# Self-attention over four 64x64 images on one Trainium2 core: the next image's v loaded by halves of a unit over 26 steps instead of by units over 16

## The chip, the cores and the metric

One core of one Trainium2 chip. The metric is the device time in microseconds from launch to end, the median of several runs. Nothing else runs on the chip beside it.

## The reference, cut to what matters

The input `x` has the shape (4, 64, 64, 256): four images, N = 4096 positions, C = 256 channels, all float32.

```python
q = einsum('bwhc,cd->bwhd', x, Wq) + bq        # 128 channels
k = einsum('bwhc,cd->bwhd', x, Wk) + bk        # 128 channels
v = einsum('bwhc,cd->bwhd', x, Wv) + bv        # 256 channels
pq, pk, pv = (t.reshape(B, -1, N) for t in (q, k, v))
energy = einsum('bcn,bcm->bnm', pq, pk)        # 4096 x 4096 for each image
attention = softmax(energy, axis=-1)
out = einsum('bcm,bnm->bcn', pv, attention).reshape(B, W, H, C)
return gamma * out + x
```

## The kernel before, in words

The order of all the work is written out by hand. After a prologue that projects image 0, one loop runs over n = 0 to 511. A step n stands for image b = n // 128, group g = (n % 128) // 16 (512 of the 4096 columns n of the reference) and unit t = n % 16 (256 of the 4096 rows m). So an image has 8 groups of 16 steps, and all 16 units of v are used once in each group, in the order of t.

**Precision.** Every operand of a large product is cut into three float32r forms h, l and d, and each product is three matmul passes. So k, q and v are stored as three forms each.

**What a step does on TensorE.** `cross(n + 2)` (line 369) begins the energies of two steps ahead, `attend(n, 0)` (line 443) multiplies the first 128 channels of v's unit t with the exponentials of step n, `energy(n + 2)` (line 384) finishes the energies, and `attend(n, 1)` does the other 128 channels. The results gather in four PSUM banks, a0, b0, a1 and b1, over the 16 steps of a group. Beside it ScalarE makes the exponentials (387) and the h forms (393), and VectorE the l and d forms (419, 421) and the row sums (404).

**The next image's projection** is spread over the same loop while there is a next image: `step(p, engine)` does the piece of one of 8 pairs of tiles. Its k, q and v forms are stored to DRAM (`kf`, `qd`, `vf`) on SP's queue by `store()`. During image 3 there is nothing left to project.

**Where v lives.** `vall` holds all 16 units of one image in SBUF: unit t has two halves i, each 128 partitions x 3 forms x 256 channels. When an image ends, its units are overwritten one by one with those of the next image out of `vf`, by `load_v` on GpSimd's queue. One half is 384 KB. Unit t of the old image is last read in step 128b - 16 + t, and unit t of the new image first in step 128b + t.

**Other transfers on GpSimd's queue.** `load_k(n + 5)` (line 356), 384 KB in each step, into one of three buffers: it waits for TensorE to be done with the buffer's old content, which is `energy(n + 2)` of the same step, and is read by `cross(n + 5)`, three steps later. `load_q` (350), 768 KB at t = 8. And line 502: at t = 10 of the next group it adds the input to the finished output tile `o` with an accumulating transfer.

**How a group ends.** In the last step of a group, t = 15, `emptied(n, 0)` (line 463) copies a0 and b0 out of PSUM into the tile `o`, ScalarE's work; the two others follow in the next step. `o` has one buffer. `finish` is a generator that is advanced once in each step and carries `o` through the next group: row sums through DRAM and back (SP's queue, lines 469 to 495), the division (498), the accumulating load of x (502) and the store to `out` (505, SP's queue). So `emptied` of one group waits until the store of the group before has landed, and the next group's first `attend` waits until `emptied` has freed the banks.

The loads of v stand at the end of a step, behind that step's `load_k` in GpSimd's queue, and ahead of `proceed()`, which advances `finish`:

```python
            if n >= STEPS - NU + 3 and (n - 3) // NU % NG == NG - 1 and (n - 3) // STEPS + 1 < B:
                load_v((n - 3) // STEPS + 1, (n - 3) % NU)
            proceed()
```

So both halves of unit t are issued at the end of step 128b - 13 + t, three steps after the last use of the old unit and 13 steps ahead of the first use of the new one.

Of the kernel before, what the change touches and what calls it, by code (L numbers as in the profile page):

```python
# [20 lines left out]
def kernel(  # L21
# [36 lines left out]
    nc = tc.nc  # L58
    B, W, H, C = x.shape
# [24 lines left out]
    NG = N // NB  # L84
    NU = NM // 2
    STEPS = NG * NU
# [14 lines left out]
    with ExitStack() as fast:  # L101
# [14 lines left out]
        vall = qkv.tile([P, NU, 2, 3, C], F32R, tag="v", name="v")  # L116
# [28 lines left out]
        qd, kf, vf, units, loads, now = {}, {}, {}, {}, {}, {}  # L145
        active, stores = [], []

        def proceed():
            for pieces in list(active):
                if next(pieces, StopIteration) is StopIteration:  # L150
                    active.remove(pieces)
# [29 lines left out]
        def image(b):  # L181
            for g in range(NG):
                qd[b, g] = dram.tile([P, NJ, 3, P], F32, tag=f"qd{g}", name=f"qd_{b}_{g}")
            for t in range(NU):
                kf[b, t] = dram.tile([P, 2, 3, P], F32, tag=f"kf{t}", name=f"kf_{b}_{t}")
                vf[b, t] = dram.tile([P, 2, 3, C], F32, tag=f"vf{t}", name=f"vf_{b}_{t}")
# [13 lines left out]
        def load_x(b, i):  # L200
            if b == B or i >= NI:
                return
            if b == 0:
                t = xs4[:, i % 4]
                if i:
                    nc.sync.dma_start(t, xv[b, i])
                loads["x", b, i] = t
                return
            pair = work.tile([P, 2, 2, XB], F32, tag="xd", name=f"x_{b}_{i}", bufs=1)
            for u in range(2):  # L210
                nc.sync.dma_start(pair[:, u], xv[b, i + u])
                loads["x", b, i + u] = pair[:, u]
# [120 lines left out]
        def store():  # L333
            for to, f in stores:
                if to.dtype == F32R:
                    nc.gpsimd.dma_start(to, f)
                else:
                    nc.sync.dma_start(to, f.bitcast(F32))
            stores.clear()

        def load_v(b, t):
            for i in range(2):
                nc.gpsimd.dma_start(vall[:, t, i], vf[b, t][:, i])  # L343

        def q_tile(g, name, dtype=F32R):
            return work.tile([P, NJ, 3, P], dtype, tag=f"q{g % 2}", name=name, bufs=1)
# [1 line left out]
        def load_q(b, g):  # L348
            loads["q", b, g] = q_tile(g, f"q_{b}_{g}")
            nc.gpsimd.dma_start(loads["q", b, g], qd[b, g])  # L350

        def load_k(n):
            b, u = divmod(n, STEPS)
            if b < B:
                t = kpool.tile([P, 2, 3, P], F32R, tag="k", name=f"k_{b}_{u}")
                nc.gpsimd.dma_start(t, kf[b, u % NU])  # L356
                loads["k", n] = t
# [5 lines left out]
        def cross(n):  # L363

            if n >= B * STEPS:
                return
            for i in range(2):
                e = units["e", n, i] = ps_e.tile([P, NB], F32, tag="e", name=f"e_{n}_{i}")
                nc.tensor.matmul(e, *forms(n, i, 2), start=True, stop=False, skip_group_check=True)  # L369
                nc.scalar.mul(e, e, -REST)  # L370

        def energy(n):

            if n >= B * STEPS:
                return
            if n % NU:
                x = ppool.tile([P, 2, NB], F32, tag="x", name=f"x_{n}")
            else:
                x = ppool.tile([P, 2, NB], F32, tag="s", name=f"s_{n // NU}")
            units[n] = x  # L380
            for i in range(2):
                e = units.pop(("e", n, i))
                for f in range(2):
                    nc.tensor.matmul(  # L384
                        e, *forms(n, i, f), start=False, stop=(f == 1), skip_group_check=True
                    )
                nc.scalar.activation(x[:, i, :], e, AF.Exp, scale=(1.0 + E) ** 3 / E)  # L387

        def upper(n):
            if n >= B * STEPS:  # L390
                return
            h = ppool.tile([P, 2, NB], F32R, tag="h", name=f"h_{n}", bufs=3)
            nc.scalar.activation(h, units[n], AF.Identity, scale=UPPER)  # L393
            units[n] = units[n], h
# [36 lines left out]
        def attend(n, j, order=(0, 1, 2)):  # L431

            t = n % NU
            if t == 0:
                for i, c in enumerate("ab"):
                    pool, tag = ps_o, f"{c}{j}"
                    if j and n >= (B - 1) * STEPS and n // NU % 2 == 0:
                        pool, tag = now["banks"][i]
                    now[c, j] = pool.tile([P, NB], F32, tag=tag, name=f"{c}{j}_{n // NU}")
            for f in order:  # L440
                to = now["ab"[f == 2], j]
                for i in (1, 0) if f == 1 else (0, 1):
                    nc.tensor.matmul(  # L443
                        to,
                        vall[:, t, i, f, j * P : (j + 1) * P],
                        units[n][f][:, i, :],
                        start=(t == 0 and i == 0 and f != 1),
                        stop=(t == NU - 1 and f != 0 and i == f // 2),
                        skip_group_check=True,
                    )  # L450

        def emptied(n, j, banks=None, only=None, vector=False):

            if j == 0:
                now["o"] = work.tile([P, 2, 2, NB], F32, tag="o", name=f"o_{n // NU}", bufs=1)
            for c, scale in enumerate((gam2, gam1)):
                if only in (None, c):
                    y = banks[c] if banks else now["ab"[c], j]
                    to = now["o"][:, c, j, :]
                    if vector:  # L460
                        nc.vector.tensor_scalar(to, y, scale, None, ALU.mult)
                    else:
                        nc.scalar.activation(to, y, AF.Identity, scale=scale)  # L463
# [230 lines left out]
        for n in range(B * STEPS):  # L694
            b, u = divmod(n, STEPS)
            g, t = divmod(u, NU)
            final = n == B * STEPS - 1
            if n == 0:
                image(1)
                load_x(1, 0)  # L700
            if u == STEPS - 5 and b + 2 < B:
                image(b + 2)
            if n == B * STEPS - 6:
                xr = ppool.tile([P, 2, NB], F32, tag="s", name="xr")
                nc.sync.dma_start(xr, xg[b, g])
            cross(n + LOOK)
            turn = t == NU - 1 and not final
            if t == 0 and n:
                upper(n + LOOK - 1)
            p = n - 2 + (n > 17)  # L710
            step(p, "act")
            late = n >= (B - 1) * STEPS
            if not final:
                attend(n, 0)
            if late and 1 <= t <= 2 and n > 1:
                emptied(n - 1 - t, 1, done, t - 1)
            energy(n + LOOK)
            load_k(n + LOOK + 3)
            store()
            if t == 0 and n:  # L720
                done = full
            if turn:
                emptied(n, 0)
            else:
                upper(n + LOOK)
            step(p, "pe")
            if turn:
                active.append(finish(n // NU, now["o"], now["s"]))
            if t == 0 and n and not late:
                emptied(n - 1, 1, done, vector=True)  # L730
            halves(n + 1)
            step(p, "dve")
            if final:
                finish_last(n, xr)
                break
            attend(n, 1)
            full = now["a", 1], now["b", 1]
            if n == 17:
                for engine in ("act", "pe", "dve"):
                    step(p + 1, engine)  # L740
            if t == 8 and n + NU < B * STEPS:
                load_q(*divmod(n // NU + 1, NG))
            if n >= STEPS - NU + 3 and (n - 3) // NU % NG == NG - 1 and (n - 3) // STEPS + 1 < B:
                load_v((n - 3) // STEPS + 1, (n - 3) % NU)
            proceed()

    NB = 512
    NG = N // NB
    NJ = NB // P
    NP = NM // 2  # L750
    with tc.If(nc.values_load(again[0:1, 0:1]) > 0), ExitStack() as general:
# [91 lines left out]
        for b in range(B):  # L843
# [16 lines left out]
            for g in range(NG):  # L860
# [65 lines left out]
                r = work.tile([P, NB], F32, tag="r", name=f"gr_{b}_{g}")  # L926
# [36 lines left out]
```

## Time and profile before

| | |
|---|---|
| median of 3 runs | 2329.9 us (2328.8 to 2330.72) |
| the profiled execution's own time | 2329.92 us |
| its span, first to last instruction | 2328.0 us |
| PE / DVE / ACT / POOL busy | 99% / 93% / 77% / 18% of the span |
| granted TensorE clock | 0.999 |
| bytes moved by DMA | 445.30 MB, mean 191 GB/s |

PE is TensorE, PEld its weight loads, DVE VectorE, ACT ScalarE, POOL GpSimd and SP SyncE, which issues transfers only. In rows of the views, `x5` is a count, and an arrow in brackets tells the idle time just before an instruction and what ended it. A view of windows gives each engine's busy time in a stretch of the span. "Landing" of a transfer is the time from its issue until its semaphore tells that all bytes are there. The DMA share is the mean busy share of the 16 DMA engines; it can exceed 1, as packets overlap.

### The profile page before, as it was taken

How to read it: one execution, taken by the hardware profiler on the slowest of the kernel's cores; microseconds unless marked ns; L12 is line 12 of the kernel's file. 1: busy time of each engine (PE TensorE's matmuls, PEld its weight loads, DVE VectorE, ACT ScalarE, POOL GpSimd, SP SyncE). 2: the span in 40 equal slices, each digit the busy share in tenths (PEclk: the TensorE clock that was granted, in tenths of full speed). 3: DMA queues.
4: the chain of work that ended last, by engine and by line, in shares of the span. 5: the costliest groups of instructions: out<-in, count | busy, mean ns of one | idle time of the engine just before them, and what ended most of it. 6: DMA issues, size and time to landing. Idle time of an engine off the chain costs nothing.

```text
span 2328.0 us, 31989 instructions
## 1 busy us (share of the span) xinstructions
PE 2309.8 (99%) x10758; PEld 1934.2 (83%) x10758; DVE 2175.0 (93%) x2174; ACT 1797.0 (77%) x2917; POOL 417.3 (18%) x716
## 2 busy tenths in 40 slices
PE   9999999999999999999999999999999999999998
PEld 9888888888878888888888888888887888888887
DVE  8999999999999999999999999999999999888988
ACT  7778777787777777777777777777787788788875
POOL 7111111111321111111132111111113111111110
PEclk9999999999999999999999999999999999999999
DMA  8567765577985776666698567665579745545553
GB/s 266 162 168 210 205 177 155 168 208 200 298 249 167 208 203 180 166 168 195 201 319 246 167 188 206 198 167 167 169 226 332 206 135 142 146 133 149 154 151 97
DMA packets 232190, 445.30 MB, mean 191 GB/s; under 512 B 27986, under 2 KB 109652, under 8 KB 232020
## 3 DMA queue, kind: packets, MB, share of 16 engines
q0 software_dynamic: 101120, 280.54, 45.0%
q1 hardware_dynamic: 130352, 162.38, 20.9%
q8 instruction: 88, 1.44, 0.3%
q14 instruction: 82, 0.67, 0.1%
q10 hardware_dynamic: 548, 0.26, 0.0%
HBM read 321.92 MB, written 120.39 MB: 190 GB/s over the span
## 4 chain that ended last, share of the span: by engine, by line
PE 96%; DMA 3%; ACT 0%; DVE 0%; issue 0%; POOL 0%; ACTq 0%; DVEq 0%
PE a L443 39%; PE e L384 19%; PE b L443 19%; PE e L369 10%; PE qv L257 5%; PE v L274 3%; PE xt L219 1%; DMA out_dram<-o 1%; DMA o<-in_x_dram 1%; DMA k<-kf 1%; DMA rows<-in_L_conv_bk_dram 0%; ACT qv L292 0%; POOL v L343 0%; ACT o L463 0%; POOL k L356 0%
## 5 line engine op out<-in xcount | busy, mean ns | idle before, releaser
L387 ACT ACTIVATE x<-e 128x512 f32<-128x512 f32 x960 | 522.1, 596 | 323.2 <-PE e L384 323.1
L370 ACT ACTIVATE e<-e 128x512 f32<-128x512 f32 x1024 | 546.4, 571 | 135.3 <-PE e L369 135.3
L443 PE MATMUL a<-h,v 128*128 128x512 f32 x2048 | 634.6, 391 | 4.6 <-ACT o L463 4.6
L443 PE MATMUL a<-ld,v 128*128 128x512 f32 x2048 | 631.7, 390 | 0.0
L443 PE MATMUL b<-ld,v 128*128 128x512 f32 x2048 | 631.6, 390 | 0.0
L419 DVE TENSOR_TENSOR ld<-x,h 128x1024 fp32r<-128x1024 f32 x480 | 586.1, 1221 | 37.0 <-ACT h L393 21.0
L404 DVE TENSOR_TENSOR s<-s,x 128x1024 f32<-128x1024 f32 x480 | 585.6, 1220 | 35.2 <-ACT x L387 34.0
L356 POOL DMA_DIRECT2D k<-kf x512 | 272.4, 532 | 1847.9 <-PE e L384 1753.1
L421 DVE SCALAR_TENSOR_TENSOR ld<-h,x 128x1024 fp32r<-128x1024 f32 x480 | 585.6, 1220 | 0.0
L384 PE MATMUL e<-q,k 128*128 128x512 f32 x2048 | 548.1, 390 | 0.0
L393 ACT ACTIVATE h<-x 128x1024 fp32r<-128x1024 f32 x480 | 510.6, 1064 | 14.2
L443 PEld LDWEIGHTS a<-ld,v 128*128 128x128 f32 x2048 | 384.8, 188 | 80.3
L443 PEld LDWEIGHTS b<-ld,v 128*128 128x128 f32 x2048 | 384.7, 188 | 80.0 <-DVE ld L421 0.2
L384 PEld LDWEIGHTS e<-q,k 128*128 128x128 f32 x2048 | 384.6, 188 | 79.4
L443 PEld LDWEIGHTS a<-h,v 128*128 128x128 f32 x2048 | 379.8, 188 | 79.3 <-ACT o L463 5.5
L369 PE MATMUL e<-q,k 128*128 128x512 f32 x1024 | 316.2, 390 | 2.5 <-DMA k<-kf 2.5
L369 PEld LDWEIGHTS e<-q,k 128*128 128x128 f32 x1024 | 191.7, 188 | 43.3 <-ACT o L463 1.8
L310 DVE SCALAR_TENSOR_TENSOR f<-f,qv 128x512 fp32r<-128x512 f32 x128 | 86.1, 683 | 0.3
L419 DVE TENSOR_TENSOR ld<-s,h 128x1024 fp32r<-128x1024 f32 x32 | 39.2, 1226 | 46.6 <-ACT h L393 46.6
L257 PE MATMUL qv<-wf,xf 128*128 128x256 f32 x576 | 78.2, 287 | 0.2
L257 PEld LDWEIGHTS qv<-wf,xf 128*128 128x128 f32 x576 | 74.7, 193 | 3.1 <-issue 0.9
L165 DVE SCALAR_TENSOR_TENSOR vf<-vf,v 128x512 fp32r<-128x512 f32 x96 | 65.4, 682 | 0.5 <-ACT vf L155 0.4
(88 smaller groups left out, 1129.2 us busy)
## 6 DMA issues: line engine op xcount, KB each, us to landing
k<-kf POOLq DMA_DIRECT2D x512, 384.0 KB, 3.6
vf<-vf SPq DMA_DIRECT2D x96, 384.0 KB, 5.2
v<-vf POOLq DMA_DIRECT2D x96, 384.0 KB, 8.3
kf<-f SPq DMA_DIRECT2D x128, 192.0 KB, 3.6
qd<-f SPq DMA_DIRECT2D x124, 192.0 KB, 3.8
q<-qd POOLq DMA_DIRECT2D x31, 768.0 KB, 6.2
zd<-s SPq DMA_DIRECT2D x62, 256.0 KB, 4.9
y<-zd SPq DMA_DIRECT2D x248, 64.0 KB, 4.4
```

What stands on the lines that cost most here:

```text
L257: nc.tensor.matmul(to[:, s, :], left, right.rearrange("p s a -> p (s a)") if w else right, start=(f == 2 and s == k == 0), stop=(f == 1 an ...
L310: nc.vector.scalar_tensor_tensor(f[:, :, :, j, :], h.bitcast(F32), s, y, ALU.mult, op)
L356: nc.gpsimd.dma_start(t, kf[b, u % NU])
L369: nc.tensor.matmul(e, *forms(n, i, 2), start=True, stop=False, skip_group_check=True)
L370: nc.scalar.mul(e, e, -REST)
L384: nc.tensor.matmul(e, *forms(n, i, f), start=False, stop=(f == 1), skip_group_check=True)
L387: nc.scalar.activation(x[:, i, :], e, AF.Exp, scale=(1.0 + E) ** 3 / E)
L393: nc.scalar.activation(h, units[n], AF.Identity, scale=UPPER)
L404: nc.vector.tensor_tensor(s, s, x, ALU.add)
L419: nc.vector.tensor_tensor(l, x, h.bitcast(F32), ALU.subtract)
L421: nc.vector.scalar_tensor_tensor(d, h.bitcast(F32), 1.0 + E, x, ALU.mult, ALU.subtract)
L443: nc.tensor.matmul(to, vall[:, t, i, f, j * P : (j + 1) * P], units[n][f][:, i, :], start=(t == 0 and i == 0 and f != 1), stop=(t == NU - ...
```

## The change

`load_v` takes one half instead of a unit. Number the 32 halves m = 0 to 31, unit m // 2, half m % 2. Half m is now issued at the end of step 128b - 13 + (13 m // 16). The first half stands where it stood; the last, m = 31, stands at the end of step 128b + 12, which is t = 12 of the new image's first group, three steps ahead of its use at t = 15. A step issues one or two halves, 32 in 26 steps, where it was two in each of 16 steps. The number of transfers and their sizes stay: 96 of 384 KB for the three image changes. They keep their place within the step.

```diff
-        def load_v(b, t):
-            for i in range(2):
-                nc.gpsimd.dma_start(vall[:, t, i], vf[b, t][:, i])
+        def load_v(b, t, i):
+            nc.gpsimd.dma_start(vall[:, t, i], vf[b, t][:, i])
...
-            if n >= STEPS - NU + 3 and (n - 3) // NU % NG == NG - 1 and (n - 3) // STEPS + 1 < B:
-                load_v((n - 3) // STEPS + 1, (n - 3) % NU)
+            for m in range(2 * NU):
+                c, r = divmod(n + NU - 3 - 13 * m // 16, STEPS)
+                if r == 0 and 0 < c < B:
+                    load_v(c, m // 2, m % 2)
             proceed()
```

Line numbers below are those of the kernel before; behind `load_v` the changed kernel's are one lower.

## The prediction

> **What bounds the kernel now.** I read the page first.
>
> ```profile
> PE 2309.8 (99%) x10758; PEld 1934.2 (83%) x10758; DVE 2175.0 (93%) x2174; ACT 1797.0 (77%) x2917; POOL 417.3 (18%) x716
> ...
> GB/s 266 162 168 210 205 177 155 168 208 200 298 249 167 208 203 180 166 168 195 201 319 246 167 188 206 198 167 167 169 226 332 206 135 142 146 133 149 154 151 97
> ```
>
> TensorE is busy for 99% of the span, so a change of transfers can win back only TensorE's few gaps, or open new ones. The second row is the rate in fortieths of the span. It stands out in three places, slices 11, 21 and 31, the ends of images 0, 1 and 2, where v is loaded. So I went there with the windows view, one window for one group of 16 steps, cut at the first matmul of its first step.
>
> ```profile
> core 0: us, PE busy (x) PEld busy (x) DVE busy (x) ACT busy (x) POOL busy (x), PEclk, DMA share, GB/s
> 496.58:568.39 71.81, 71.81 (x334) 60.06 (x333) 68.61 (x70) 55.75 (x92) 10.16 (x18) 1.00 0.65 183
> 640.20:715.02 74.82, 72.15 (x334) 59.98 (x332) 68.85 (x70) 56.39 (x92) 14.01 (x26) 1.00 0.84 255
> 1217.71:1291.84 74.13, 72.16 (x333) 59.91 (x332) 68.89 (x70) 56.38 (x92) 14.04 (x26) 1.00 0.84 258
> 1786.38:1855.12 68.74, 66.22 (x289) 53.81 (x288) 59.79 (x55) 52.44 (x85) 15.48 (x28) 1.00 0.82 253
> 1855.12:1920.40 65.28, 65.28 (x289) 54.12 (x288) 59.11 (x54) 52.03 (x85) 10.15 (x18) 1.00 0.53 145
> ```
>
> An undisturbed group takes 71.81 us while a next image is projected and 65.28 us in image 3. The groups at the start of images 1, 2 and 3 take 74.82, 74.13 and 68.74 us with the same matmuls. The image changes thus lose 3.01, 2.32 and 3.46 us, together **8.79 us**. Who makes TensorE wait there is told by the waits of the whole span (us in total, times, longest):
>
> ```profile
> ACT o L463 <- DMA out_dram<-o: 5.4, 2, 3.1
> ...
> PE a L443 <- ACT o L463: 4.6, 2, 2.7
> ...
> PE e L369 <- DMA k<-kf: 2.5, 3, 1.4
> ```
>
> There are two sorts. At the first two changes the copy of the finished banks into `o` waits for the last group's store to land, and TensorE waits for the copy. At the third the copy is in time, and TensorE waits for k. Both are late transfers. How late the first one is, ScalarE's timeline tells, and how the transfers stand to their ordinary times, the table of transfers (last column: median us to landing):
>
> ```profile
> 642.74 0.69 ACT L463 ACTIVATE o<-a,gam 128x512 f32<-128x512 f32 x1 [3.07 <-DMA out_dram<-o]
> ```
>
> ```profile
> k<-kf POOLq DMA_DIRECT2D x512, 384.0 KB, 3.6
> ...
> out_dram<-o SPq DMA_DIRECT2D x31, 512.0 KB, 5.2
> ```
>
> Below are, by line and window, the store at the first change, then v early in the first change and late in it, then k at the third.
>
> ```profile
> L505 SPq DMA_DIRECT2D out_dram<-o x1: 593/593/593, 628.5 to 628.5; - x1
> ...
> DMA to landing us min/median/max: 14.2/14.2/14.2
> ```
>
> ```profile
> L343 POOL DMA_DIRECT2D v<-vf x8: 536/548/561, 585.2 to 598.0; - x8
> ...
> DMA to landing us min/median/max: 3.8/4.3/4.6
> ```
>
> ```profile
> L343 POOL DMA_DIRECT2D v<-vf x10: 538/553/578, 621.3 to 640.3; - x10
> ...
> DMA to landing us min/median/max: 10.4/11.5/13.7
> ```
>
> ```profile
> L356 POOL DMA_DIRECT2D k<-kf x5: 528/531/533, 1789.6 to 1809.3; - x5
> ...
> DMA to landing us min/median/max: 7.0/10.6/12.2
> ```
>
> The first loads of v land in 4.3 us, those 35 us later in 11.5, and k, which needs 3.6 us elsewhere, in 10.6. The store takes 14.2 us where 5.2 is usual. Nothing in these transfers differs but the time at which they are issued: work has piled up ahead of them. The rates say so too.
>
> ```profile
> 480.00:489.00 9.00, 9.00 (x41) 7.46 (x40) 8.20 (x9) 7.00 (x12) 1.06 (x2) 1.00 0.86 283
> 585.00:597.00 12.00, 12.00 (x57) 10.03 (x56) 12.00 (x13) 9.10 (x16) 4.54 (x10) 1.00 0.91 275
> 642.00:651.00 9.00, 7.52 (x37) 6.33 (x38) 7.56 (x8) 7.45 (x13) 2.13 (x5) 1.00 1.11 396
> ```
>
> At 642 to 651 us the engines are full, and move 396 GB/s. That is the most I take them to do.
>
> **Part one: less traffic at a time.** A step is 71.81 / 16 = 4.49 us on average. Two halves are 2 x 393,216 bytes, so v asks for 786,432 / 4.49 = 175 GB/s before; after, 32 halves in 26 steps are 1.23 in a step, 108 GB/s. The busiest stretch of an undisturbed group, 480 to 489 us, carries 283 GB/s without v. With v it comes to 458 GB/s before, above 396, so a backlog grows; after, 391, just under it. So after the change a backlog can form only for moments within a burst.
>
> The same as a count of what stands ahead of the late transfers: one half at 396 GB/s is 0.99 us of all engines' time. At the first change the store is issued 628.5 us into the span, ten steps after v began. By then 2 x 10 = 20 halves were issued before; after, those with 13 m // 16 up to 9, m = 0 to 12, which is 13. Seven halves fewer are 6.9 us less work. ScalarE needs the store only 3.07 us earlier, and of the store's 14.2 us some 9.0 lie above its usual 5.2. So the store should be in time by about 3.8 us, and what TensorE waits for next is what it waits for in every undisturbed group: nothing. The second change has the same order of work and a smaller loss. At the third, k's 10.6 us less 6.9 is 3.7, next to the ordinary 3.6. When does k have to be there? The rows of a step:
>
> ```profile
> 632.04 0.62 PE L369 MATMUL e<-q,k 128*128 128x512 f32 x2
> 632.49 0.62 PE L443 MATMUL a<-h,v 128*128 128x512 f32 x2
> 632.94 0.62 PE L443 MATMUL a<-ld,v 128*128 128x512 f32 x2
> ...
> 636.12 0.61 PE L369 MATMUL e<-q,k 128*128 128x512 f32 x2
> ```
>
> ```profile
> 635.22 0.53 POOL L356 DMA_DIRECT2D k<-kf  x1 [3.40 <-PE e L384]
> 635.74 1.08 POOL L343 DMA_DIRECT2D v<-vf  x2
> ```
>
> A short step is 636.12 - 632.04 = 4.08 us; k is issued 635.22 - 632.04 = 3.18 us into it, and read at the start of the third step after, so it has 3 x 4.08 - 3.18 = 9.06 us. The 10.6 and 12.2 of the third change exceed that; 3.7, even 6, do not. All three losses go: **-8.79 us**.
>
> **Part two: less lead for the last units.** Both halves of a unit had 13 steps; now the lead shrinks to 3 for the last half (the two before it have 4). It is issued 635.74 - 632.04 = 3.70 us into a step, and read 632.49 - 632.04 = 0.45 us into the third after, behind `cross`: 3 x 4.08 + 0.45 - 3.70 = 8.99 us in image 3, where steps are shortest, and more in images 1 and 2. The price is zero if it lands within 4.3 us (the rows of the unfilled engines), or 13.7 - 8.99 = 4.7 us for each change if it takes the 13.7 of full engines. I take zero: 391 GB/s at the worst stretch is nearer to the state at 585 to 597 us, 275 GB/s with 3.8 to 4.6 us, than to a lasting backlog, and up to 8.99 us is free. What hides it is the three steps of attention.
>
> [...]
>
> **Part three: small change on the queues.** The 96 issues stay, about 0.55 us of GpSimd each, behind the same `load_k`. GpSimd is 18% busy. The step that issued two now mostly issues one, so the accumulating load and the next k are up to 0.5 us earlier in the queue; for the ten added steps of each change an issue stands behind `load_k`, with nothing behind it until the next k, whose buffer comes free only a step later. No queue of SP is passed. The changed kernel's listing shows that TensorE's first matmul on a half now often waits for that half's own semaphore (60 places, 3 before) where an earlier wait covered it. In the rows above, line 369's pair of matmuls at 632.04, which waits for k and for ScalarE, both met by then, takes 0.45 us until the next pair starts, and line 443's at 632.49, with no wait of its own, 0.45 too; so zero, within 0.01 us x 57 = 0.6 us either way.
>
> **Sum.** Against the profiled execution's own 2329.92 us, which is the median of the three runs within 0.02: 2329.92 - 8.79 = **2321.1 us**, 0.38% less. No more than 8.79 can be won, as TensorE has no other gap in these stretches.
>
> **The rivals.** *One sort of wait stays.* The store moves on SP's queue and k on GpSimd's, and the engines may share themselves out so that only one profits. If k's waits stay at the third change, 2329.92 - 3.01 - 2.32 = 2324.6 us; if the store's stay, 2329.92 - 3.46 = 2326.5. For it: 391 is close to 396, and the store lies behind other stores of its queue. [...] Against: the store needs only a third of its excess removed.
>
> *It does nothing.* If the projection's own stores and loads fill the engines in these stretches, v's share does not decide: 2329.9. Against: the group at 496.58 has the same of these and no gap.
>
> *Slower: the full stretch only gets longer.* If the engines stay full from the burst until v ends at t = 12, the old waits stay, and the last half lands after TensorE wants it: 4.7 us in image 3. In images 1 and 2 some of the steps are longer, so no more than 4.7 each. Together up to 2329.92 + 3 x 4.7 = 2344.0 us. It decides from a landing of 8.99 us on at t = 12. For it: 13.7 us have been seen. Against: the rate after v has stretched stays below 396, and the engines caught up before.
>
> **How the numbers follow.** Forecast, all three losses gone but for a microsecond: 0.75. K's waits stay: 0.10, the store's stay: 0.04, nothing: 0.03, slower: 0.08. A measurement can tell about 0.2%, 4.7 us, from no change. Faster by more than that, below 2325.2, are the forecast and the case of k's waits, 0.85; within it the store's case and no effect, 0.07; slower 0.08. The range starts 1.1 us below the forecast, the spread of the three runs downwards, at 2320.0, and reaches 2325.0, over most of the case of k's waits, which leaves out under 2 in 10.
>
> **What would show it.** Right: the groups that start images 1, 2 and 3 take 71.8, 71.8 and 65.3 us; the wait of ScalarE's copy for the store and of line 369's matmul for k are gone; the store at the first change lands in 6 to 9 us; v's late loads, 11.5 us before, land in 4 to 7 us, and no half takes over 9; the rate in slices 11, 21 and 31 is lower, and those behind higher. Wrong: a wait of TensorE for v at t = 15 of an image's first group, or windows with 390 GB/s after the image change.

## The result, and the profile after

| | before | after |
|---|---|---|
| median of 6 runs each | 2329.95 us (2327.78 to 2330.72) | 2319.81 us (2319.64 to 2321.3) |
| the profiled execution's own time | 2329.92 us | 2319.64 us |
| its span | 2328.0 us | 2317.9 us |
| ratio of the times | | 0.996, 95% interval 0.9949 to 0.9971 |

The kernel is 10.1 us faster, 0.4%. The forecast was 2321.1 us, a gain of 8.8. Line numbers of the changed kernel are one lower from line 344 on, so line 442 is `attend`, 383 `energy`, 368 `cross`, 462 the copy into `o`, 504 the store.

First the windows over the groups that start images 1, 2 and 3, cut as in the prediction:

```profile
core 0: us, PE busy (x) PEld busy (x) DVE busy (x) ACT busy (x) POOL busy (x), PEclk, DMA share, GB/s
638.90:710.71 71.81, 71.81 (x333) 60.01 (x332) 68.59 (x70) 55.73 (x92) 18.87 (x35) 1.00 0.93 283
1213.41:1285.22 71.81, 71.81 (x333) 60.01 (x332) 68.60 (x70) 55.86 (x92) 18.90 (x35) 1.00 0.92 282
1779.76:1845.04 65.28, 65.28 (x290) 54.05 (x289) 59.66 (x55) 52.12 (x85) 20.27 (x37) 1.00 0.95 283
```

They take 71.81, 71.81 and 65.28 us, as long as undisturbed groups; before, it was 74.82, 74.13 and 68.74. (For image 3 both the prediction's window and this one begin two steps ahead of the group, which changes nothing in the difference.) This is all that TensorE still waits for in the whole span:

```profile
engine line waited for: us in total, times, longest us
PE wp L140 <- DVE ones L132: 1.1, 1, 1.1
PE qv L257 <- DVE qv L285: 0.4, 1, 0.4
PE qv L257 <- DVE xf L165: 0.4, 1, 0.4
PE xt L219 <- DMA xs<-in_x_dram: 0.2, 1, 0.2
PE qv L257 <- ACT qv L292: 0.2, 1, 0.2
```

All of it lies in the prologue. The waits for the copy into `o` and for k are gone. The transfers behind them, by line and window: the store at the first image change, v late in it, and k at the third.

```profile
L504 SPq DMA_DIRECT2D out_dram<-o x1: 592/592/592, 625.9 to 625.9; - x1
...
DMA to landing us min/median/max: 9.6/9.6/9.6
```

```profile
L342 POOL DMA_DIRECT2D v<-vf x8: 536/543/578, 620.0 to 643.1; - x8
...
DMA to landing us min/median/max: 6.7/7.6/8.9
```

```profile
L355 POOL DMA_DIRECT2D k<-kf x5: 531/533/536, 1782.9 to 1799.3; - x5
...
DMA to landing us min/median/max: 3.6/5.8/6.4
```

The store lands in 9.6 us instead of 14.2, v in 7.6 instead of 11.5, k in 5.8 instead of 10.6. And the rates, just after the image change, in the nine microseconds behind that, and in the burst of the new image's first group, where v's last halves are issued:

```profile
640.70:649.70 9.00, 9.00 (x45) 7.55 (x44) 8.68 (x9) 7.25 (x12) 2.66 (x5) 1.00 1.15 360
649.70:658.70 9.00, 9.00 (x42) 7.44 (x41) 8.74 (x9) 7.13 (x13) 2.14 (x4) 1.00 0.95 251
694.00:703.00 9.00, 9.00 (x41) 7.46 (x40) 8.19 (x9) 6.96 (x13) 1.59 (x3) 1.00 1.12 363
```

The engines are still nearly full in the first and the last of these windows, 360 GB/s and a share above 1.1, but nine microseconds after the image change they are down to 251 GB/s, so they no longer fall behind for long enough to make anything late.

### The profile page after: what moved, and what is told of

Read it like the earlier page. It is cut to its first block, busy times and chain, and to the rows that moved or that the text cites. A ratio compares the mean times of both kernels' runs of the same rounds, so it can differ in the third digit from the quotient of the medians.

```text
span 2317.9 us, 31970 instructions
## 1 busy us (share of the span) xinstructions
PE 2307.0 (100%) x10758; PEld 1931.5 (83%) x10758; DVE 2174.3 (94%) x2174; ACT 1796.9 (78%) x2917; POOL 417.1 (18%) x716
## 4 chain that ended last, share of the span: by engine, by line
PE 99%; DVE 0%; ACT 0%; DMA 0%; issue 0%; ACTq 0%; DVEq 0%
PE a L442 40%; PE e L383 20%; PE b L442 20%; PE e L368 10%; PE qv L257 5%; PE v L274 3%; PE xt L219 1%; DMA raw<-in_L_conv_Wk_dram 0%; ACT qv L292 0%; DVE xf L165 0%; PE zp L517 0%; DVE o_last L547 0%; DVE o_last L542 0%; DVE qv L285 0%; DVE o_last L548 0%
```

## The experiments

The theory to be tested is that the loads of v, added to a group's own burst, made the store and k late. The rivals to it were that halving, not spreading, does it; that leaving the old image's last group does it; that the loads cost something still; and that the lead has no price, or a higher one.

**Whole units, spread over 26 steps.**

```diff
-                c, r = divmod(n + NU - 3 - 13 * m // 16, STEPS)
+                c, r = divmod(n + NU - 3 - 13 * (m - m % 2) // 16, STEPS)
```

> Whole units again, two halves issued together, but spread over 26 steps (the step of the unit's first half). Theory, that the rate decides: by the late store's issue 14 halves are ahead of it (13 in the change, 20 before), so all three gaps stay away: the groups that start images 1, 2 and 3 take 71.81, 71.81 and 65.28 us and the time is that of the change, 2319.8 us within 1. Rival, that it is the halving that decides, because k or the store no longer stand behind two halves in a row: at least a third of the 8.8 us comes back, 2322.5 us or more.

Measured: 2320.22 us, ratio to before 0.9961 (0.9947 to 0.9975). The three groups take 71.81, 71.82 and 65.28 us; the store at the first change lands in 10.3 us. The halves are not what matters; the spreading is.

**No load of v.**

```diff
-                if r == 0 and 0 < c < B:
+                if r == 0 and 0 < c < 0:
```

> No load of a next image's v at all (images 1 to 3 are computed with the v of image 0, 37.7 MB less is moved). Theory, that the change has taken away all that these loads cost: the same as the change, 2319.8 us within 1.5, and no group shorter than 71.81 or 65.28 us. Rival, that the loads still cost something that the groups do not show, for instance slower engines: below 2317 us.

Measured: 2320.03 us, 0.9958 (0.9941 to 0.9974), the same as the change.

```profile
639.33:711.15 71.82, 71.82 (x334) 60.01 (x332) 68.62 (x70) 55.81 (x92) 10.20 (x18) 1.00 0.64 183
1213.84:1285.65 71.81, 71.81 (x333) 60.01 (x332) 68.61 (x70) 55.78 (x92) 10.20 (x18) 1.00 0.66 184
1780.18:1845.46 65.28, 65.28 (x289) 54.05 (x288) 59.66 (x55) 52.10 (x85) 10.20 (x18) 1.00 0.59 165
```

The rate is 183 GB/s instead of 283, and the groups take as long as with the change, to within a hundredth of a microsecond. After the change v's transfers are thus wholly hidden, and no other schedule of them can gain more.

**Over 20 steps.**

```diff
-                c, r = divmod(n + NU - 3 - 13 * m // 16, STEPS)
+                c, r = divmod(n + NU - 3 - 10 * m // 16, STEPS)
```

> Halves over 20 steps (10 m // 16): v asks for 140 GB/s, with the burst's 283 it is 423, above the 396 of full engines. Theory that counts the work ahead: at the store's issue 16 halves against 20, 4.0 us less where 3.07 was wanted, and k's 10.6 us become 6.6 where 9.06 are to be had: all or nearly all gaps gone, 2319.8 to 2321 us. Rival, that any rate above full leads to the same full state: about half of the 8.8 us comes back, 2324 us.

Measured: 2323.2 us, 0.9975 (0.9964 to 0.9987).

```profile
639.11:711.38 72.27, 72.16 (x334) 59.93 (x332) 68.86 (x70) 56.40 (x92) 16.18 (x30) 1.00 0.90 273
1214.07:1287.42 73.35, 72.17 (x333) 59.95 (x332) 68.85 (x70) 56.39 (x92) 16.17 (x30) 1.00 0.89 270
1781.96:1847.86 65.90, 65.57 (x290) 53.98 (x288) 59.69 (x55) 52.29 (x85) 17.62 (x32) 1.00 0.91 279
```

Losses of 0.46, 1.54 and 0.62 us remain, 2.6 in all, which lies in between the two expectations. My count was too kind: four halves fewer ahead of the store were to bring it 4.0 us earlier, but at the first change it still took 12.9 us to land.

**Two halves a step, ten steps later.**

```diff
-                c, r = divmod(n + NU - 3 - 13 * m // 16, STEPS)
+                c, r = divmod(n + 3 - m // 2, STEPS)
```

> Two halves in each of 16 steps as before, but ten steps later, from step 128b - 3 to 128b + 12; the last half has the same three steps of lead as in the change. Theory, that the rate over the burst of transfers within a group decides: the backlog moves into the first group of the new image, its store lands late, and the copy into o waits 2 to 3 us at the end of that group, so that the second group of images 1 and 2 takes 73 to 75 us; the last unit of v is 1 to 2 us late as well. Image 3 has no projection beside it and loses under 1. Together 2325 to 2329 us. Rival, that only the last group of the old image is critical, and moving the loads out of it is what gained: 2319.8 us.

Measured: 2322.68 us, 0.9969 (0.9957 to 0.9982). Neither came out. The store of the old image's last group lands in 5.0 us, the ordinary time (5.2 in the median before), so keeping v away from that store gains most of the 10.1 us. The new first group's store makes nobody wait either. What is left, 2.7 us, is TensorE's wait for v itself, all of it in the first groups of images 1 and 2, at t = 11, 14 and 15:

```profile
639.04:713.04 74.00, 72.90 (x333) 59.77 (x332) 68.77 (x70) 55.86 (x92) 24.74 (x46) 1.00 1.06 330
713.04:784.85 71.81, 71.81 (x333) 60.01 (x332) 68.61 (x70) 55.77 (x92) 10.19 (x18) 1.00 0.65 189
```

```profile
L342 POOL DMA_DIRECT2D v<-vf x10: 538/551/558, 680.0 to 699.2; - x10
...
  PEld a L442: 2.6, 4
  PE a L442: 1.0, 2
...
DMA to landing us min/median/max: 7.8/9.2/12.1
```

The first two rows are the first two groups of image 1; the two indented rows of the second view tell who waited for these loads. Up to 12.1 us to landing is more than three steps of lead give (8.99 us for three short steps, somewhat more here, where steps are longer). So the burst at t = 9 to 15 is where v meets the group's own transfers, in the new image's first group (360 GB/s at 685 to 694 us) as in the old one's last. Only what is late is different, because this time v has the least to spare.

**Dodging the bursts, at three halves a step.**

```diff
-                c, r = divmod(n + NU - 3 - 13 * m // 16, STEPS)
+                at = m // 2 if m < 12 else 15 + (m - 12) // 3
+                c, r = divmod(n + NU - 3 - at, STEPS)
```

> The loads dodge the transfers of a group's steps t = 9 to 15 and t = 0, 1: two halves a step at t = 3 to 8 of the old image's last group (12 halves), none until t = 2 of the new image, then three a step until t = 8. At three a step v asks for 262 GB/s, more than the 175 before. Theory, corrected after the loads in 16 later steps: what counts is the sum of v and the group's own burst, so v in quiet steps may be fast: no gap, 2319.8 us within 1, the last group's store lands in 5 to 6 us. Rival, v's own rate counts, as the prediction put it: k and the first use of v are late behind three halves a step, 2322 us or more.

Measured: 2322.43 us, 0.9966 (0.9954 to 0.9979). At the first two changes the corrected theory holds: the groups take 71.81 us, and at the first change the store lands in 5.3 us and all of v in 3.7 to 8.0, though v's own rate is half as high again as before the change. At the third the group takes 67.97 us, with a new wait at its t = 11 (from the waits of 1822 to 1842 us):

```profile
DVE o L497 <- DMA o<-rd: 3.5, 1, 3.5
PEld a L442 <- DVE ld L418: 2.1, 1, 2.1
PE a L442 <- DVE ld L418: 1.7, 1, 1.7
```

The row sums of the group before come back through DRAM in two short transfers. Here both are late: the first, 2 KB, takes 6.5 us to land where 1.4 is the median of this run, and the second 7.1 where 4.8 is. VectorE waits for them, and behind that wait in VectorE's order stand the l forms that TensorE wants. In image 3, where steps are 4.08 us, three halves a step are 289 GB/s. That v delayed them is inferred: its last halves were under way at that time, and in no other run is there such a wait. The total is what the rival expected, 2322 us or more, but by neither of the transfers that it named. So the late transfer can be any of four: the store, k, v, or the row sums.

**One step of lead, and two.**

```diff
-                c, r = divmod(n + NU - 3 - 13 * m // 16, STEPS)
+                c, r = divmod(n + NU - 3 - 14 * m // 16, STEPS)
```

> Halves over 28 steps (14 m // 16): the last half is issued one step ahead of its use, 4.08 + 0.45 - 3.70 = 0.83 us, the two before it two steps ahead, 4.9 us. Theory, that lead has a price only once a landing exceeds it: TensorE waits for v at t = 14 or 15 of each image's first group for 3 to 6 us, 9 to 18 us in all, 2329 to 2338 us, with no other gap. Rival, that v's wait hides in slack elsewhere (TensorE makes up for it): 2319.8 us.

Measured: 2345.97 us, 1.0068 (1.0051 to 1.0085): 24.4 us in the groups, more than either expected. With two steps (`27 * m // 32`):

> Halves over 27 steps (27 m // 32): the last half is issued two steps ahead of its use, 2 x 4.08 + 0.45 - 3.70 = 4.9 us or a little more. Loads at that place landed in 6 to 8 us in the runs so far, so TensorE waits 1 to 3 us for v at t = 15 of each image's first group. Theory, that a wait's price is its length as long as it is short: 3 to 8 us in all, 2323 to 2328 us, with a granted clock of 1.00 beside the wait. Rival, that the clock falls as it did with one step of lead (0.53 for some 6 us behind waits of 5 us): 3 us more for each image change, 2330 us and above.

Measured: 2329.56 us, 0.9997 (0.9987 to 1.0006), the whole gain lost: TensorE's waits for v take 6.9 us in the three changes, 3.1 us the longest, and the groups lose 5.0, 2.7 and 1.7, together 9.4. In both runs a part is the granted clock. Windows of the run with one step of lead, the wait, then the matmuls behind it, then the next:

```profile
708.00:715.00 7.00, 2.02 (x8) 1.13 (x6) 2.96 (x3) 2.41 (x4) 1.06 (x2) 0.91 1.04 382
715.00:721.00 6.00, 5.94 (x15) 4.68 (x16) 0.10 (x1) 2.29 (x4) 0.53 (x1) 0.53 0.45 136
721.00:729.00 8.00, 8.00 (x41) 6.70 (x40) 7.77 (x8) 6.43 (x12) 1.06 (x2) 1.00 0.31 91
```

and with two:

```profile
711.00:713.00 2.00, 2.00 (x8) 1.57 (x9) 0.00 (x0) 0.00 (x0) 0.00 (x0) 0.84 0.85 333
713.00:715.00 2.00, 2.00 (x6) 1.62 (x5) 0.00 (x0) 1.56 (x3) 0.53 (x1) 0.50 0.43 161
```

With one step of lead, TensorE does 15 matmuls in the 6 us at a clock of 0.53, against 41 in the 8 us after. So the second part of the expectation for two steps, that a short wait leaves the clock alone, fell for the longest of its three waits. The place was right, t = 14 or 15 of the first group; the price is the wait and, at times, slow matmuls beside it: in the first two of these rows the lower clock took 0.09 x 7.00 + 0.47 x 6.00 = 3.5 us, at the first change with one step of lead. The half issued two steps ahead took 9.3 us to land at the first change; the change gives it a step more.

**The third image change alone.**

```diff
-                c, r = divmod(n + NU - 3 - 13 * m // 16, STEPS)
+                at = 13 * m // 16 if n > 2 * STEPS + NU else m // 2
+                c, r = divmod(n + NU - 3 - at, STEPS)
```

> The change for the last image change alone; the first two load two halves a step over 16 steps as before. Theory, that the three image changes are independent: the groups that start images 1 and 2 take about 74.8 and 74.1 us, that of image 3 65.28, and the time is that of the change plus 5.3 us, 2325 us. Rival, that a delay once begun is carried on or that the waits share a cause elsewhere: all three as in the one or the other kernel.

Measured in a single run: 2326.62 us.

```profile
639.01:715.21 76.20, 73.70 (x334) 61.12 (x332) 69.08 (x70) 56.55 (x92) 14.06 (x26) 0.98 0.82 249
1217.90:1292.23 74.33, 72.54 (x334) 59.97 (x333) 68.96 (x70) 56.44 (x92) 14.07 (x26) 1.00 0.85 256
1786.76:1852.04 65.28, 65.28 (x290) 54.05 (x288) 59.67 (x55) 52.13 (x85) 20.24 (x37) 1.00 0.96 280
```

As far as a single run tells, the changes are independent: the third is free, and the other two cost 4.4 and 2.5 us, where 3.0 and 2.3 were expected. The first shows a mean clock of 0.98: behind a wait of 2.5 us the clock was 0.55 in the next 3 us and 0.88 in the 3 us after them.

**The kernel before, twice more.**

> The kernel before, unchanged, for a second look at where its time goes. The change gained 10.1 us where the gaps of the profiled execution sum up to 8.79. Theory A, the clock: waits of 2.5 us and more of TensorE lower the granted clock in some executions (0.55 for 3 us behind a wait of 2.5 us in the run with the last image alone, 1.00 behind the 2.67 us of the first profile), so the three image changes cost 9 to 11 us here and a window behind one of the waits shows a clock of 0.5 to 0.9. Theory B, the start: the first step begins 1.3 us later in the kernel before (37.82 us against 36.55); then it begins at 37.5 us or later here as well and the image changes cost 8.8 us again.

> The kernel before once more, the same question. Theory A: image changes of 9 to 11 us together, spread over a microsecond or more between the looks, first step at 36.5 to 37 us. Theory B: first step at 37.5 us or later, image changes of 8.8 us.

Measured, in a single run each: 2327.5 and 2333.16 us. The image changes cost 2.62 + 1.97 + 2.77 = 7.4 us in the one and 4.23 + 3.03 + 3.17 = 10.4 in the other, with 8.8 in the first profile. Line 369's first matmul, which still lies in the prologue, began at 36.9 and 39.0 us, with 37.8 in the first profile and 36.5 in the changed kernel's. Both theories hold a part. In the costlier run the clock fell behind the first wait, of 2.33 us:

```profile
642.00:645.00 3.00, 0.71 (x3) 0.62 (x4) 1.41 (x3) 1.46 (x3) 0.04 (x1) 1.00 1.10 398
645.00:648.40 3.40, 3.40 (x10) 2.65 (x9) 2.74 (x3) 2.40 (x5) 0.00 (x0) 0.51 1.11 389
648.40:651.00 2.60, 2.60 (x12) 2.10 (x12) 2.60 (x3) 2.52 (x4) 1.60 (x3) 0.99 1.11 396
```

## Why the prediction was right, step by step

- **The three losses, 8.79 us: right.** The groups came down to 71.81, 71.81 and 65.28 us to the hundredth. That the loss was v's and nothing else's is shown by the run without v's loads, where it is gone as well, and which is no faster than the change.
- **The size, 10.1 instead of 8.8 us: a term missing.** The sum took one execution's gaps for fixed. They cost 7.4, 8.8 and 10.4 us in three profiled runs, in part because the clock fell behind a wait in the costliest of them (0.51 in the second row above). The range's lower end, 2320.0, rested on the spread of three runs of the kernel before, and the median measured lies 0.2 us under it. The profiled pair differs by 10.1 us of span: 8.8 at the image changes and 1.3 in the prologue, which the change doesn't touch. There the clock was half in the first profile (first line) and full in the changed kernel's (second line):

```profile
7.40:10.80 3.40, 3.40 (x19) 3.40 (x18) 3.00 (x6) 1.23 (x3) 1.77 (x4) 0.50 0.40 125
7.40:10.80 3.40, 2.99 (x26) 2.80 (x24) 3.38 (x6) 1.67 (x4) 0.83 (x4) 1.00 0.46 145
```

Over the nine kernels with the changed code and its variants, line 368's first matmul began at 36.5 to 38.1 us, and over the three runs of the kernel before, at 36.9 to 39.0. The two overlap, so the 1.3 us is taken for chance. A gain of 8.8 us also lies within the interval of the ratio, which is 6.8 to 11.9 us. That the gaps are 8.8 us on average is not shown; three profiles are too few.
- **The count of work ahead, 0.99 us for each half: right in direction, wrong as a rule.** The store at the first change landed 14.2 us after its issue with 20 halves ahead, 12.9 with 16 (20 steps), 10.3 and 9.6 with 14 and 13 (26 steps), 5.0 to 5.3 where none or two came within the burst. From 16 to 13 it wins 3.3 us, from 20 to 16 only 1.3, where the first four halves were to bring 4.0. With 12 ahead, in the runs with one and two steps of lead, it took 10.2 and 10.1, and at the second change 16 halves took 12.9 us and 20 took 12.3. In the change the forecast margin of 3.8 us was 2.9: the store landed at 635.5 us; before, ScalarE wanted it at 639.67, and the changed execution is 1.3 us ahead by then. The landing became 4.6 us shorter, not 6.9. Some 1.3 us more came from an earlier issue (625.9 instead of 628.5 us, less the 1.3 us by which the execution is ahead), which the count had left out. So the outcome was right partly by a margin wide enough to bear a wrong term.
- **k at the third change: mis-sized, without consequence.** Forecast 3.7 us, measured 5.8, to be had 9.06.
- **v's landing: mis-sized, the price right.** The forecast was 4 to 7 us for v's late loads and none over 9. The eight of 620 to 643 us took 7.6 us in the median, and the longest of all 96 took 9.3, at the second change, issued four steps ahead of its use. The last half itself took 7.0, 7.2 and 6.8 us at the three changes, where at least 8.99 were to be had. The price was zero as said, and the runs with less lead show that it rests on the third step: at two steps the whole gain goes.
- **The rate: right.** 391 GB/s was worked out for the worst stretch, and 360 and 363 were measured behind the image change and in the new burst, under 396. In the slices 11, 21 and 31 of the span the rate fell from 298, 319 and 332 GB/s to 266, 292 and 289, and in those behind them it rose from 249, 246 and 206 to 268, 267 and 258.
- **The rivals.** One sort of wait alone stayed in no run at 26 steps. That the full stretch gets longer and v is late came true where the 16 steps were moved back by ten, by 2.2 us in image 1, and did not in the change. With one step of lead the price is 24 us; with three steps the lead has none, as TensorE never waits for v, and the earlier issue, with 13, was the dearer one by 10.1 us.

## What to carry to other kernels

When a prefetch has slack, spend it: spread its transfers until the sum of it and the periodic burst stays under the most that the engines were seen to move (here 391 GB/s against 396), and stop while the shortest lead still exceeds the landings that the spread state shows (here 8.99 us and more against 7.2 at most for the last half). Look for the late transfer not in the prefetch but in those with the least slack, here a store into a single-buffered tile and k with 9 us. And test against a run without the transfer at all: where that is no faster, nothing more can be gained from this transfer.

## What the runs showed of the hardware that was not expected

One short wait of TensorE cost nearly twice its length, and a slightly longer one hardly more than itself. Behind a wait of 2.50 us in the run with the third change alone, the granted clock was 0.55 in the next 3 us and 0.88 in the 3 us after them (the first three lines), and the group lost 4.4 us. Behind one of 2.67 us in the first profile the clock stayed at 1.00 (the last three lines), and the group lost 3.0.

```profile
639.00:642.00 3.00, 0.62 (x3) 0.19 (x1) 0.58 (x1) 0.62 (x2) 0.70 (x2) 1.00 1.11 397
642.00:645.00 3.00, 2.88 (x7) 2.33 (x8) 2.34 (x4) 2.59 (x5) 0.00 (x0) 0.55 1.11 393
645.00:648.00 3.00, 3.00 (x13) 2.40 (x13) 3.00 (x3) 2.16 (x4) 1.45 (x3) 0.88 1.11 392
640.00:643.00 3.00, 0.81 (x4) 0.35 (x2) 0.22 (x1) 0.26 (x1) 0.90 (x2) 1.00 1.12 398
643.00:646.00 3.00, 2.52 (x11) 2.11 (x12) 2.34 (x4) 3.00 (x6) 0.00 (x0) 1.00 1.10 394
646.00:649.00 3.00, 3.00 (x15) 2.48 (x14) 3.00 (x3) 2.95 (x5) 1.59 (x3) 1.00 1.12 394
```

So it depends on more than the length of the wait. The two further runs of the kernel before agree: behind the wait of 2.33 us in the costlier one the clock was 0.51 for 3.4 us, and in the other, where the longest wait for the copy into `o` was 2.3 us as well, the mean clock of all three groups is 1.00. Behind the wait of 3.09 us in the run with two steps of lead it was 0.84, 0.50 and 0.80 in three windows of 2 us. On what else it depends is not shown by these runs.
